# A new order for the steps of the attention section of a fused attention and feed-forward block

## The chip, the cores and the metric

The kernel runs on one core of one Trainium2 chip. The metric is the time of one execution on the device in microseconds (us); lower is better. Times of one kernel are given as the median of several runs. A profile is a record of one further execution.

## The reference

Input x has 32 sequences of 64 tokens with 1024 features (2048 tokens), in float32. The block is an attention layer followed by a feed-forward layer, each with a conditioning layer ahead of it:

```
x = x + attn(cond(x, itok_B_0_2))       # cond: W plus a low-rank delta chosen per sequence
x = x + ffn(cond2(x, itok_B_0_7))       # cond2 and ffn: a base matrix plus top-2 of 8 low-rank experts
```

What matters here is `attn`, with 32 query heads and 8 key and value heads of width 32:

```
qkv = x @ w_qkv.T + b_qkv
q, k, v = split(qkv);  q, k = rope(q), rope(k);  k, v repeated 4 times
scores = q @ k.T / sqrt(32), masked causally
out = softmax(scores) @ v
return out @ w_o.T + b_o
```

## The kernel before

The 2048 tokens are worked on in two halves of 1024 (`hf` 0 and 1); the code is the same for both. Activations lie with features on the 128 partitions and tokens along the free axis. Large matrix products are done in seven block products where eight would be usual (Strassen's scheme in Winograd's form). A `Group` (line 213 on) is one such product of 256 output features by 1024 tokens. It owns three PSUM banks x, y and z, and its steps are:

- on TensorE (PE): `m1` and `m2` into x; `m6`, `m7` and `m4` into y; `p5` and `m3` into z. With the long inner dimension (`qk` groups) a step is four matmuls of 128x512, with the short one (`o` groups) two. In the trace a float32 matmul is two records, so eight or four.
- between them the banks are read: `e1` (ScalarE, ACT) copies x after `m1`; `e6` and `e7` (VectorE, DVE) add y to that copy after `m6` and `m7`, before the next product is added into y; `out11` reads z after `p5` and before `m3`; `out00`, `out01` and `out10` read the finished x, z and y.

The section that the change touches lies at the end of attention: the last `qk` groups (g = 5 holds the values; `held` is the group before it, whose last output is still open), and the first half of the output projection (`o_pairs`, `pairs[0]` to `pairs[3]`). Woven into these are eight units of attention (`u` = 0 to 7, one of two head groups with one of four sets of sequences), each with a chain of steps over two half units (`two` = 0, 1):

- `scores(u)`: 32 small matmuls on 32x32 tiles of TensorE (L1383) into four banks; `flipped(u, two)`: DVE transposes two banks into a tile `e` (L1409); `shaded`: POOL (GpSimd) adds the mask (L1416); `topped`: DVE takes the maxima (L1428); `lowered`: POOL subtracts a maximum (L1433); `exponentials`: ACT (L1446, L1449); `totalled`: DVE sums and takes reciprocals (L1454, L1455); `divided`: POOL multiplies (L1460); `turned`: DVE transposes the weights (L1472) into a tile that `in_place_of(j)` takes over from the column sums of `x`.
- `v_turned(c, i)`: four transposes of the values on TensorE (L1364), and `v_out`: ACT copies them; `values(us)`: 64 small matmuls (L1483, tiles `av`) for two units; `valued_out`: four copies on ACT (L1498) into `q`.
- `o_sums`: column sums on DVE for the projection; `to_x[...].pop(...)()`: POOL adds a result to x; `o_load(G, p)`: four transfers of projection weights on SP's queue. `g.some`, `held.out01` and the `more` in an `out` issue the low-rank matmuls of L434 on 32 rows.

The whole section stands in `with tc.manual_schedule()`: each engine's queue, that of PE, DVE, ACT, POOL and SP, has its instructions in the order of the calls. Semaphores guard the data between engines, and an engine that waits holds up all that is queued behind it. `ps_tile` is a pool of five PSUM banks (scores, `av`, some banks of groups), `group_bank` one of three.

A matmul step and a read-out, and the place of the tile that `turned` writes:

```
def m6(self):
    self.y = self.bank("y")
    self.mult(self.y, "s2", "t2", True)
def e6(self):
    self.add01 = self.sum("u1")
    nc.vector.tensor_add(self.add01, self.y, self.add10)
...
def in_place_of(j, name):
    return xt.pool.tile([P, 4, 512], F32, tag=f"sum{j - 1}", name=f"{name}_{hf}")
```

Of the kernel before, what the change touches and what calls it, by code (L numbers as in the profile page):

```python
# [77 lines left out]
def block_kernel(ctx: ExitStack, tc: tile.TileContext, a, out: bass.AP):  # L78
# [1176 lines left out]
    for hf in range(2):  # L1255
# [212 lines left out]
        def turned(u, two, j=None):  # L1468
            if two == 0:
                to = in_place_of(j, f"ws{u}").rearrange("p j k -> p (j k)")[:, : 48 * HB]  # L1470
                ws[u] = to, to.rearrange("p (j m k) -> p j m k", j=4, m=4)
            nc.vector.transpose(ws[u][0][:, two * 24 * HB : (two + 1) * 24 * HB], units[u][two])  # L1472
# [111 lines left out]
        with tc.manual_schedule():  # L1584
# [42 lines left out]
            flipped(2, 1)  # L1627
            topped(2, 0)
            shaded(2, 1)
            topped(2, 1)  # L1630
# [3 lines left out]
            scored[3] = scores(3)  # L1634
            g.e7()
            g.some((0, 0), (1, 0), held=held)
            turned(1, 0, 3)
            turned(1, 1)
            flipped(3, 0)
            g.m4()  # L1640
            exponentials(2, (0,))
            exponentials(2, (1,))
            flipped(3, 1)
            totalled(2, 0)
            g.out(0, 0, g.x, None)
            shaded(3, 0)
            totalled(2, 1)
            shaded(3, 1)
            topped(3, 0)
            g.part("p5", (0, 1))  # L1650
            g.part("p5", (2, 3))
            divided(2, 1)
            lowered(3, 0)
            exponentials(3, (0,))
            g.out10()
# [12 lines left out]
            wo0 = o_load(0, 0)  # L1668
            rotated()
            turned(2, 0, 4)  # L1670
            totalled(3, 0)
            turned(2, 1)
            totalled(3, 1)
            divided(3, 0)
            g.part("p3", (0, 1))
            g.some((0, 1))
            g.part("p3", (2, 3))
            valued_out((0, 1))
            g.out01()
            scored[4] = scores(4)  # L1680
            v_turned(1, 0, group_bank)
            v_turned(1, 1, group_bank)
            divided(3, 1)
            turned(3, 0, 1)
            flipped(4, 0)
            flipped(4, 1)
            turned(3, 1)
            shaded(4, 0)
            shaded(4, 1)
            topped(4, 0)  # L1690
            topped(4, 1)
            lowered(4, 1)
            v_out(1, 0)
# [5 lines left out]
            v_out(1, 1)  # L1699
            pairs[0].m1()  # L1700
            pairs[0].e1()
            values((2, 3))
# [24 lines left out]
            pairs += o_pairs(0, 1, wo1, ot, (group_bank, group_bank), to_x[1])  # L1727
            pairs[0].e6()
            totalled(4, 1)
            divided(4, 1)  # L1730
            topped(5, 0)
            pairs[1].out00()
            pairs[2].m1()
            scored[6] = scores(6)
            pairs[0].m7()
            pairs[0].p5()
# [4 lines left out]
            o_sums(0, t0, 0, (3,))  # L1741
            o_sums(0, t0, 1, (3,))
            shaded(5, 1)
            lowered(5, 0)
            topped(5, 1)
            exponentials(5, (0,))
            totalled(5, 0)
            divided(5, 0)
            lowered(5, 1)
            pairs[0].m3()  # L1750
            pairs[0].out01()
            pairs[2].e1()
            exponentials(5, (1,))
            flipped(6, 0)
            pairs[0].m4()
# [11 lines left out]
            pairs[1].m7()  # L1767
            flipped(7, 0)
            turned(5, 1)
            flipped(7, 1)  # L1770
            topped(6, 0)
            shaded(6, 1)
            pairs[1].e7()
            pairs[1].out11()
            topped(6, 1)
            shaded(7, 0)
            to_x[0].pop((0, 1, 0))()
            lowered(6, 1)
            topped(7, 0)
# [5 lines left out]
            pairs[1].out10()  # L1785
            pairs[1].out01()
            shaded(7, 1)
            to_x[0].pop((0, 0, 1))()
            lowered(6, 0)
            exponentials(6, (0,))  # L1790
            totalled(6, 0)
            pairs[2].p5()
            pairs[2].e6()
            pairs[2].m7()
            divided(6, 0)
            to_x[0].pop((0, 1, 1))()
            turned(6, 0, 4)
            pairs[2].e7()
            wo0 = o_load(1, 0)
            pairs[3].m1()  # L1800
            lowered(7, 0)
            exponentials(6, (1,))
            exponentials(7, (0,))
            topped(7, 1)
            lowered(7, 1)
            exponentials(7, (1,))
            pairs[3].e1()
            valued_out((4, 5))
            pairs[2].out11()
            totalled(6, 1)  # L1810
            pairs[2].m4()
            pairs[2].m3()
            pairs[2].out10()
            pairs[3].m6()
            totalled(7, 0)
            divided(6, 1)
            divided(7, 0)
            pairs[3].e6()
            pairs[2].out01()
            totalled(7, 1)  # L1820
            pairs[3].m2()
            pairs[3].out00()
            turned(6, 1)
            turned(7, 0, 1)
            pairs[3].p5()
            pairs[3].m7()
            to_x[0].pop((1, 0, 1))()
            divided(7, 1)
            turned(7, 1)
            values((6, 7))  # L1830
# [9 lines left out]
            o_sums(1, t1, 1, (0,))  # L1840
            o_sums(1, t1, 0, (1,))
            o_sums(1, t1, 1, (2,))
            o_sums(1, t1, 1, (1,))
            pairs[3].out01()
            o_sums(1, t1, 1, (3,))
            pairs[3].out10()
            o_sums(1, t1, 0, (3,))
            to_x[1].pop((0, 0, 1))()
            to_x[1].pop((1, 0, 1))()
            to_x[1].pop((0, 1, 0))()  # L1850
            to_x[1].pop((0, 1, 1))()
            to_x[0].pop((1, 1, 0))()
            to_x[0].pop((1, 1, 1))()
            to_x[1].pop((1, 1, 0))()
            to_x[1].pop((1, 1, 1))()
# [372 lines left out]
```

## Time and profile before

| what | us |
|---|---|
| median of 4 runs (lowest to highest) | 1128.46 (1127.76 to 1128.64) |
| the profiled execution, its own time | 1128.69 |
| its span, first to last instruction | 1126.8 |
| TensorE busy in the span | 1115.6 |
| the section in half one, roughly 410 to 546: PE, DVE, POOL, ACT busy of 136 | 135.0, 98.6, 85.9, 51.9 |
| the section in half two, roughly 836 to 975: PE, DVE, POOL, ACT busy of 139 | 136.5, 98.3, 84.0, 51.8 |
| granted TensorE clock over the span | 1.00 |

Busy time is that of instructions at work, without waiting. PEld is the weight load of TensorE, which overlaps its matmuls. In a list of waits a line names who waited, for whom, the total in us, how often, and the longest. In a timeline a line has the start and length in us, the engine, the source line, the operation, output and inputs by tile names, the shape, the number of records, and in brackets the engine's idle time ahead of it with what ended it. "issue" stands where no semaphore explains the wait.

### The profile page before, as it was taken

The page shows a single profiled execution, that of the slowest core. Times are in us where ns is not written, and L with a number is a line of the kernel's source. Part 1 is how long each engine was busy: PE and PEld are TensorE (multiplying, and loading weights), DVE is VectorE, ACT ScalarE, POOL GpSimd, SP SyncE. Part 2 cuts the span into 40 slices and gives each one's busy share as a digit, 9 for nine tenths or more (in the row PEclk, how much of TensorE's full clock was granted, in tenths as well). Part 3 has the DMA queues.
Part 4 walks back from the last instruction along what each step waited for, and adds up shares of the span by engine and source line. Part 5 has one row for each costly group of instructions (what it writes and reads, how often), then busy time and mean ns, then how long its engine had stood idle before and what let it go on. Part 6 is the DMA issues. An engine that isn't in the chain of part 4 may idle for free.

```text
span 1126.8 us, 15708 instructions
## 1 busy us (share of the span) xinstructions
PE 1115.6 (99%) x5974; PEld 625.5 (56%) x5974; DVE 721.0 (64%) x1279; ACT 191.3 (17%) x736; POOL 549.9 (49%) x530
## 2 busy tenths in 40 slices
PE   9999999999999999999999999999999999999998
PEld 4555555555444444444458887444444444458887
DVE  4879853749445787973946565344767864847654
ACT  1101001000000426450000000000225550011000
POOL 5877586550532665647405651111545556602333
PEclk9999999999999999999999999999999999999999
DMA  9312773969322232032116669222222024113454
GB/s 321 122 38 94 284 248 135 337 210 323 118 74 75 75 113 77 8 123 98 33 48 194 202 193 310 77 75 75 75 75 76 2 76 135 50 36 98 148 150 145
DMA packets 115147, 144.99 MB, mean 129 GB/s; under 512 B 6912, under 2 KB 92928, under 8 KB 113024
## 3 DMA queue, kind: packets, MB, share of 16 engines
q1 hardware_dynamic: 103168, 113.99, 31.3%
q0 software_dynamic: 4848, 19.93, 5.0%
q10 hardware_dynamic: 7056, 10.07, 2.5%
q8 instruction: 47, 0.77, 0.3%
q14 instruction: 28, 0.23, 0.1%
HBM read 102.97 MB, written 41.00 MB: 128 GB/s over the span
## 4 chain that ended last, share of the span: by engine, by line
PE 96%; DVE 2%; DMA 1%; POOL 1%; issue 1%; ACTq 0%; POOLq 0%; DVEq 0%
PE qk_y L272 11%; PE o_y L272 7%; PE qk_z L272 7%; PE qk_x L272 7%; PE f_y L272 6%; PE o_x L272 5%; PE o_z L272 5%; PE cqp_y L596 4%; PE f_z L272 4%; PE f_x L272 4%; PE cf_y L272 4%; PE cqp_z L596 3%; PE cqp_x L596 3%; PE cf_z L272 2%; PE cf_x L272 2%; PE f_z L284 2%
## 5 line engine op out<-in xcount | busy, mean ns | idle before, releaser
L1302 POOL TENSOR_TENSOR t<-raw,consts 128x512 f32<-128x512 f32 x40 | 57.6, 1445 | 130.0 <-DVE q L1301 78.6
L1446 ACT ACTIVATE e<-e,top 128x64 f32<-128x64 f32 x256 | 85.2, 336 | 87.1 <-DVE top L1428 87.1
L272 PE MATMUL qk_y<-sum_x,s_qk 128*128 128x512 f32 x192 | 86.8, 595 | 0.0
L272 PE MATMUL qk_x<-x,w_qk 128*128 128x512 f32 x192 | 86.6, 594 | 0.0
L272 PE MATMUL f_y<-s_f,w_f 128*128 128x256 f32 x336 | 82.3, 380 | 0.3 <-DVE f_u L327 0.3
L1460 POOL TENSOR_TENSOR e<-e,tot 128x256 f32<-128x256 f32 x64 | 52.0, 835 | 40.9 <-DVE tot L1455 40.8
L272 PEld LDWEIGHTS f_y<-s_f,w_f 128*128 128x128 f32 x336 | 63.8, 190 | 9.3 <-DVE f_u L327 0.7
L1416 POOL TENSOR_TENSOR e<-e,consts 128x512 f32<-128x512 f32 x32 | 40.9, 1294 | 52.3 <-DVE e L1409 52.3
L272 PEld LDWEIGHTS qk_y<-sum_x,s_qk 128*128 128x128 f32 x192 | 36.1, 190 | 45.5 <-issue 43.7
L272 PEld LDWEIGHTS qk_x<-x,w_qk 128*128 128x128 f32 x192 | 36.3, 190 | 44.9 <-issue 44.4
L272 PE MATMUL o_x<-q,w_o 128*128 128x512 f32 x128 | 59.4, 598 | 0.2 <-issue 0.2
L1446 ACT ACTIVATION_READ_ACCUMULATOR e<-e,top 128x1 f32 x256 | 48.4, 189 | 0.0
L1222 POOL COPY gatesr<-oh1r 128x1024 f32<-128x1024 f32 x4 | 4.1, 1036 | 86.8 <-DVE oh1r L1220 86.8
L272 PE MATMUL qk_y<-sum_x,w_qk 128*128 128x512 f32 x96 | 44.4, 606 | 0.0
L272 PE MATMUL qk_z<-x,s_qk 128*128 128x512 f32 x96 | 43.9, 597 | 0.0
L272 PE MATMUL qk_z<-sum_x,s_qk 128*128 128x512 f32 x96 | 43.4, 595 | 0.0
L272 PEld LDWEIGHTS o_x<-q,w_o 128*128 128x128 f32 x128 | 23.7, 190 | 28.4 <-issue 27.4
L596 PE MATMUL cqp_y<-t_p,s_p 128*128 128x384 f32 x112 | 38.7, 489 | 0.5 <-POOL s_p L708 0.4
L1334 DVE SCALAR_TENSOR_TENSOR raw<-qk_z,consts,qk_u 128x512 f32<-128x512 f32 (+1 forms) x28 | 18.3, 664 | 31.8 <-PE qk_z L434 27.8
L1409 DVE STREAM_TRANSPOSE e<-sc 128x384 f32<-128x384 f32 x64 | 32.0, 550 | 9.8 <-PE sc L1383 9.4
L296 ACT COPY f_p<-f_x 128x256 f32<-128x256 f32 x28 | 10.4, 372 | 159.6 <-PE f_x L272 117.8
L1311 DVE TENSOR_TENSOR q<-q,t 128x512 f32<-128x512 f32 x32 | 31.2, 976 | 9.0 <-POOL t L1302 9.0
(407 smaller groups left out, 2414.1 us busy)
## 6 DMA issues: line engine op xcount, KB each, us to landing
w_f<-cf SPq DMA_DIRECT2D x28, 512.0 KB, 4.3
w_qk<-cqkv SPq DMA_DIRECT2D x12, 1024.0 KB, 5.5
w_f<-cf SPq DMA_DIRECT2D x28, 384.0 KB, 4.5
x<-in_xT SPq DMA_DIRECT2D x16, 512.0 KB, 5.8
w_o<-in_wo SPq DMA_DIRECT2D x16, 512.0 KB, 4.6
s_o<-wos SPq DMA_DIRECT2D x16, 512.0 KB, 5.8
sqk<-s_qk POOLq DMA_DIRECT2D x6, 1024.0 KB, 4.2
outT<-o ACTq DMA_DIRECT2D x20, 256.0 KB, 4.1
```

The costliest lines, as they stand in the source:

```text
L272: self.last = nc.tensor.matmul(ps, self.weights[left][:, kc, :], self.right(right, kc), start=first and kc == 0, stop=kc == self.h - 1, sk ...
L284: nc.tensor.matmul(ps, lhs, rhs, start=False, stop=True, skip_group_check=True)
L296: nc.scalar.copy(self.add10, self.x)
L596: nc.tensor.matmul(ps, self.weights[left][kc], self.right(right, kc), start=first and kc == 0, stop=kc == self.h - 1, skip_group_check=True,)
L1222: nc.gpsimd.tensor_copy(gates, oh1.unsqueeze(3).to_broadcast([P, NT, E, R]))
L1302: nc.gpsimd.tensor_mul(t2v, rv, c3)
L1311: nc.vector.tensor_add(*unfinished.pop())
L1334: nc.vector.scalar_tensor_tensor(to, ps, bias, add, ALU.add, ALU.add)
L1409: nc.vector.transpose(e[:, 12 * HB * i : 12 * HB * (i + 1)], scored[u][2 * two + i][:, : 12 * HB])
L1416: nc.gpsimd.tensor_add(diagonal, diagonal, upper)
L1446: nc.scalar.activation(es[1][:, n], es[1][:, n], AF.Exp, bias=top[:, 1, n : n + 1], accum_out=tot[:, 1, n : n + 1])
L1460: nc.gpsimd.tensor_mul(es[i], es[i], wide(tots[u][two][:, i], (i + 1) * HB))
```

## The change

The same calls are made in another order. Nothing else is changed: the same instructions, tiles and banks. On TensorE's queue the order changes at five places in each half:

1. `scores(2)` stands ahead of `g.m6()` instead of behind it, and `g.m2()` ahead of `flipped(2, 0)` and `g.e6()`.
2. `v_turned(0, 1)` stands next to `v_turned(0, 0)`, ahead of the low-rank matmul of `g.out11()` (in `g.some((1, 1))`).
3. `scores(5)` stands ahead of `pairs[0].m2()` and `pairs[1].m2()` instead of between them.
4. `pairs[1].p5()` stands ahead of `scores(7)` and `pairs[2].m2()`.
5. `pairs[1].m3()` stands behind `pairs[2].m6()`.

The other moves are on DVE, ACT and POOL. The diff, cut to the parts with these moves and the ones around them:

```diff
             g.m1()
+            scored[2] = scores(2)
             g.m6()
-            scored[2] = scores(2)
             g.e1()
             turned(0, 0, 2)
+            turned(0, 1)
+            g.m2()
+            flipped(2, 0)
             g.e6()
-            turned(0, 1)
-            flipped(2, 0)
-            g.m2()
+            flipped(2, 1)
             shaded(2, 0)
-            flipped(2, 1)
             topped(2, 0)
...
             v_turned(0, 0, group_bank)
+            v_turned(0, 1, ps_tile)
+            v_out(0, 0)
             held.out01()
-            v_out(0, 0)
+            v_out(0, 1)
             g.some((1, 1))
-            v_turned(0, 1, ps_tile)
             divided(2, 0)
-            g.out11()
             topped(3, 1)
             lowered(3, 1)
-            v_out(0, 1)
+            g.out11()
+            exponentials(3, (1,))
             values((0, 1))
-            exponentials(3, (1,))
+            valued_out((0, 1))
...
             valued_out((2, 3))
+            o_sums(0, t0, 0, (0,))
             o_sums(0, t0, 1, (0,))
-            o_sums(0, t0, 0, (0,))
-            o_sums(0, t0, 1, (1,))
+            o_sums(0, t0, 0, (1,))
             o_sums(0, t0, 1, (2,))
             lowered(4, 0)
+            scored[5] = scores(5)
+            o_sums(0, t0, 1, (1,))
+            pairs[1].e1()
             pairs[0].m2()
-            scored[5] = scores(5)
-            flipped(5, 0)
-            o_sums(0, t0, 0, (1,))
-            shaded(5, 0)
-            pairs[1].e1()
             pairs[1].m2()
             pairs[0].m6()
+            pairs[0].out00()
+            flipped(5, 0)
+            shaded(5, 0)
             flipped(5, 1)
-            pairs[0].out00()
...
             flipped(6, 1)
+            pairs[1].p5()
+            pairs[1].e6()
             scored[7] = scores(7)
             pairs[2].m2()
-            pairs[1].p5()
-            shaded(6, 0)
-            pairs[1].e6()
+            pairs[1].m7()
             totalled(5, 1)
...
             pairs[2].out00()
             values((4, 5))
             pairs[1].m4()
-            pairs[1].m3()
             pairs[2].m6()
             pairs[1].out10()
+            pairs[1].out11()
+            pairs[1].m3()
+            lowered(6, 0)
+            shaded(7, 0)
+            shaded(6, 1)
+            topped(6, 1)
+            pairs[2].p5()
...
             values((6, 7))
-            pairs[3].e7()
+            pairs[3].m4()
             pairs[3].out11()
-            pairs[3].m4()
+            pairs[3].out00()
             pairs[3].m3()
+            to_x[1].pop((1, 1, 1))()
```

`pairs[0].m7()`, `pairs[0].p5()`, `turned(4, 0, 4)`, `pairs[0].e7()`, `turned(4, 1)`, `pairs[0].out11()`, `o_sums(0, t0, 0, (3,))`, `o_sums(0, t0, 1, (3,))` and `shaded(5, 1)` keep their order; `pairs[0].m3()` follows them at once in the new order.

More of the change, by code (lines that the diff above doesn't have):

```diff
@@ L1636, in block_kernel @@
             g.some((0, 0), (1, 0), held=held)
+            g.m4()
             turned(1, 0, 3)
+            flipped(3, 0)
             turned(1, 1)
-            flipped(3, 0)
-            g.m4()
             exponentials(2, (0,))
+            totalled(2, 0)
+            shaded(3, 0)
             exponentials(2, (1,))
+            g.out(0, 0, g.x, None)
             flipped(3, 1)
-            totalled(2, 0)
-            g.out(0, 0, g.x, None)
-            shaded(3, 0)
             totalled(2, 1)
@@ L1651, in block_kernel @@
             g.part("p5", (2, 3))
+            lowered(3, 0)
+            g.out10()
             divided(2, 1)
-            lowered(3, 0)
             exponentials(3, (0,))
-            g.out10()
             v_turned(0, 0, group_bank)
+            v_turned(0, 1, ps_tile)
+            v_out(0, 0)
             held.out01()
-            v_out(0, 0)
+            v_out(0, 1)
             g.some((1, 1))
-            v_turned(0, 1, ps_tile)
             divided(2, 0)
-            g.out11()
             topped(3, 1)
             lowered(3, 1)
-            v_out(0, 1)
+            g.out11()
+            exponentials(3, (1,))
             values((0, 1))
-            exponentials(3, (1,))
+            valued_out((0, 1))
             wo0 = o_load(0, 0)
+            turned(2, 0, 4)
             rotated()
-            turned(2, 0, 4)
+            turned(2, 1)
             totalled(3, 0)
-            turned(2, 1)
             totalled(3, 1)
-            divided(3, 0)
             g.part("p3", (0, 1))
@@ L1677, in block_kernel @@
             g.part("p3", (2, 3))
-            valued_out((0, 1))
+            scored[4] = scores(4)
             g.out01()
-            scored[4] = scores(4)
             v_turned(1, 0, group_bank)
             v_turned(1, 1, group_bank)
+            v_out(1, 1)
+            v_out(1, 0)
+            divided(3, 0)
+            flipped(4, 0)
+            turned(3, 0, 1)
+            flipped(4, 1)
             divided(3, 1)
-            turned(3, 0, 1)
-            flipped(4, 0)
-            flipped(4, 1)
+            shaded(4, 0)
             turned(3, 1)
-            shaded(4, 0)
-            shaded(4, 1)
             topped(4, 0)
-            topped(4, 1)
-            lowered(4, 1)
-            v_out(1, 0)
             two = [in_place_of(j, f"sums_o{j}") for j in (2, 3)]
@@ L1698, in block_kernel @@
             pairs = o_pairs(0, 0, wo0, ot, (group_bank, group_bank), to_x[0])
-            v_out(1, 1)
+            shaded(4, 1)
+            topped(4, 1)
+            lowered(4, 1)
             pairs[0].m1()
@@ L1726, in block_kernel @@
             divided(4, 0)
-            pairs += o_pairs(0, 1, wo1, ot, (group_bank, group_bank), to_x[1])
+            totalled(4, 1)
             pairs[0].e6()
-            totalled(4, 1)
             divided(4, 1)
@@ L1732, in block_kernel @@
             pairs[1].out00()
+            lowered(5, 0)
+            exponentials(5, (0,))
+            pairs += o_pairs(0, 1, wo1, ot, (group_bank, group_bank), to_x[1])
             pairs[2].m1()
+            pairs[2].e1()
             scored[6] = scores(6)
@@ L1743, in block_kernel @@
             shaded(5, 1)
-            lowered(5, 0)
+            pairs[0].m3()
+            totalled(5, 0)
             topped(5, 1)
-            exponentials(5, (0,))
-            totalled(5, 0)
-            divided(5, 0)
+            pairs[0].out01()
             lowered(5, 1)
-            pairs[0].m3()
-            pairs[0].out01()
-            pairs[2].e1()
             exponentials(5, (1,))
             flipped(6, 0)
+            divided(5, 0)
+            shaded(6, 0)
             pairs[0].m4()
@@ L1766, in block_kernel @@
             turned(5, 0, 1)
-            pairs[1].m7()
             flipped(7, 0)
@@ L1770, in block_kernel @@
             flipped(7, 1)
+            pairs[1].e7()
             topped(6, 0)
[L1772 to L1779, printed above, removed]
+            shaded(7, 1)
             pairs[2].out00()
@@ L1782, in block_kernel @@
             pairs[1].m4()
-            pairs[1].m3()
             pairs[2].m6()
             pairs[1].out10()
+            pairs[1].out11()
[5 more added lines that the diff above has]
+            pairs[2].p5()
+            topped(7, 0)
+            pairs[2].e6()
+            topped(7, 1)
             pairs[1].out01()
-            shaded(7, 1)
+            pairs[2].m7()
             to_x[0].pop((0, 0, 1))()
-            lowered(6, 0)
+            to_x[0].pop((0, 1, 0))()
+            lowered(6, 1)
+            lowered(7, 0)
+            to_x[0].pop((0, 1, 1))()
+            pairs[2].e7()
+            pairs[2].out11()
+            wo0 = o_load(1, 0)
+            pairs[3].m1()
+            lowered(7, 1)
             exponentials(6, (0,))
             totalled(6, 0)
-            pairs[2].p5()
-            pairs[2].e6()
-            pairs[2].m7()
             divided(6, 0)
[L1796 to L1801, printed above, removed]
             exponentials(6, (1,))
             exponentials(7, (0,))
-            topped(7, 1)
-            lowered(7, 1)
-            exponentials(7, (1,))
             pairs[3].e1()
             valued_out((4, 5))
-            pairs[2].out11()
+            pairs[2].m4()
+            pairs[2].out10()
             totalled(6, 1)
-            pairs[2].m4()
             pairs[2].m3()
-            pairs[2].out10()
             pairs[3].m6()
             totalled(7, 0)
-            divided(6, 1)
-            divided(7, 0)
-            pairs[3].e6()
+            to_x[0].pop((1, 0, 1))()
+            exponentials(7, (1,))
+            turned(6, 0, 4)
             pairs[2].out01()
@@ L1821, in block_kernel @@
             pairs[3].m2()
-            pairs[3].out00()
+            pairs[3].p5()
+            divided(7, 0)
+            divided(6, 1)
+            turned(7, 0, 1)
+            pairs[3].e6()
+            pairs[3].m7()
             turned(6, 1)
[L1824 to L1827, printed above, removed]
             divided(7, 1)
             turned(7, 1)
+            pairs[3].e7()
             values((6, 7))
-            pairs[3].e7()
+            pairs[3].m4()
             pairs[3].out11()
-            pairs[3].m4()
+            pairs[3].out00()
             pairs[3].m3()
+            to_x[1].pop((1, 1, 1))()
             t1 = [ep.tile([P, 1024], F32, tag="e", name=f"sumo{hf}{j}") for j in range(4)]
@@ L1840, in block_kernel @@
             o_sums(1, t1, 1, (0,))
+            o_sums(1, t1, 1, (1,))
             o_sums(1, t1, 0, (1,))
-            o_sums(1, t1, 1, (2,))
-            o_sums(1, t1, 1, (1,))
+            o_sums(1, t1, 1, (3,))
             pairs[3].out01()
-            o_sums(1, t1, 1, (3,))
             pairs[3].out10()
             o_sums(1, t1, 0, (3,))
-            to_x[1].pop((0, 0, 1))()
+            o_sums(1, t1, 1, (2,))
             to_x[1].pop((1, 0, 1))()
             to_x[1].pop((0, 1, 0))()
+            to_x[1].pop((1, 1, 0))()
+            to_x[0].pop((1, 1, 1))()
+            to_x[1].pop((0, 0, 1))()
             to_x[1].pop((0, 1, 1))()
             to_x[0].pop((1, 1, 0))()
-            to_x[0].pop((1, 1, 1))()
-            to_x[1].pop((1, 1, 0))()
-            to_x[1].pop((1, 1, 1))()
             ot = Columns(o_columns(1), 512, 2, [[t[:, kc, :] for kc in range(2)] for t in t1])
```

## The prediction

> **What bounds the kernel now.** I read first the busy shares and the chain that ended last, then who TensorE waited for, then TensorE's own timeline in the two stretches that the change touches (one per half of the tokens).
>
> ```profile
> PE 1115.6 (99%) x5974; PEld 625.5 (56%) x5974; DVE 721.0 (64%) x1279; ACT 191.3 (17%) x736; POOL 549.9 (49%) x530
> ...
> q8 instruction: 47, 0.77, 0.3%
> ...
> PE 96%; DVE 2%; DMA 1%; POOL 1%; issue 1%; ACTq 0%; POOLq 0%; DVEq 0%
> ```
>
> TensorE is busy 1115.6 of 1126.8 us and is 96% of the chain. A new order neither adds nor removes a matmul, so it can win only what TensorE loses now between them. The waits of TensorE, the longest first, as totals, times and longest:
>
> ```profile
> PE o_z L272 <- DVE o_u L1570: 1.7, 2, 0.8
> PE av L1483 <- issue: 1.7, 1, 1.7
> PE idle L135 <- DVE idle L132: 1.2, 1, 1.2
> PE cqp_z L596 <- POOL s_p L702: 1.0, 1, 1.0
> ...
> PE o_x L272 <- issue: 0.2, 1, 0.2
> ```
>
> Only three of these lie in the reordered section: 1.7 + 1.7 + 0.2 = 3.6 us, 0.3% of the span. That is the ceiling of any gain. The timeline (start, length, what, records) shows where they lie; a matmul of 512 columns is two records.
>
> ```profile
> 428.87 0.60 PE L1364 MATMUL v<-consts,raw 128*128 128x128 f32 x4
> 429.40 1.12 PE L434 MATMUL qk_z<-low,b1q 32*128 32x512 f32 x2
> 430.45 0.66 PE L1364 MATMUL v<-consts,raw 128*128 128x128 f32 x4
> 431.04 2.33 PE L1483 MATMUL av<-ws,v 32*32 32x256 f32 x128
> ...
> 442.13 2.33 PE L1483 MATMUL av<-ws,v 32*32 32x256 f32 x128
> 444.39 0.70 PE L272 MATMUL o_x<-q,w_o 128*128 128x512 f32 x1
> ...
> 460.81 1.98 PE L272 MATMUL o_z<-q,s_o 128*128 128x512 f32 x4 [0.85 <-DVE o_u L1570]
> ...
> 869.05 2.19 PE L1483 MATMUL av<-ws,v 32*32 32x256 f32 x113
> 872.90 0.45 PE L1483 MATMUL av<-ws,v 32*32 32x128 f32 x15 [1.66 <-issue]
> ```
>
> Back to back, a group of four records takes 1.72 us (480.22 to 481.94) and one of eight 3.43; a group next to small tiles takes 0.10 more (411.35 to 412.56 is one block of scores, 1.21 us; the group before it runs 407.82 to 411.35 = 3.53).
>
> **The o_z wait stays.** `p5` fills a bank, `out11` (L1570) must empty it, `m3` fills it again. In the new order `m7, p5, e7, out11, m3` of `pairs[0]` stand as before, with the same second `turned(4)` ahead of `out11` on DVE. 0 us; if it went after all, -0.85 in each half.
>
> **The "issue" waits are code arriving.** Queue q8 moves 0.77 MB in 47 packets, 16 KB each; TensorE's 5974 matmul and 5974 load records with its 155 queue instructions make 12,100, so an instruction is 64 bytes and a packet 256 of them. Counted in program order, the wait of half one comes before instruction 4287 (the second weight load of an `o_x`) and that of half two near 9408: 5,121 apart, 20 packets. In the trace's DMA records a q8 packet starts at 442.90 and TensorE goes on at 445.27, 2.37 later; the other starts at 870.49 and TensorE goes on at 872.90, 2.41 later. So the next 256 instructions are usable 2.4 us after their transfer starts, and an `av` block eats 256 in 2.26 us. The cost now: 444.39 to 448.47 (two groups of four) is 4.08 against 3.63 for such groups, 0.45 lost; 869.05 to 873.28 is 4.23 against 2.26, 1.97 lost. In half two the transfer starts late because the weight loads fill the queues ahead of it:
>
> ```profile
> q1 hardware_dynamic: 333, 1.24, 94.1%
> ...
> w_o<-in_wo SPq DMA_DIRECT2D x1, 512.0 KB, 5.4
> s_o<-wos SPq DMA_DIRECT2D x1, 512.0 KB, 7.5
> ```
>
> (the DMA view cut to 866.0 to 870.4: data packets take 94%, and no code packet runs.) The Trainium skill, "Runtime: NRT & Kernel Launch", section "Instruction fetch mechanics", has 16 KiB blocks of 256 instructions, as here, but calls a crossing "mostly hidden". By it, the code term below would be 0 and my sum 0.47 lower; the rows above show 0.45 and 1.97, so the rows decide.
>
> **The change part by part, per half.** Counts of compute and DMA instructions are unchanged on every engine; only places move.
>
> (1) `scores(2)` goes ahead of `g.m6()`. The 1.21 us block only changes places, and small tiles stand between large ones as before: 0. But `e6` loses cover. `turned(0, 0)` overwrites the column sums that `m6` reads (`in_place_of(2)`), so DVE now begins it when `m6` ends, with this queue ahead of `e6`:
>
> ```profile
> 411.46 0.98 DVE L1472 STREAM_TRANSPOSE ws<-e 128x768 f32<-128x768 f32 x1 [0.36 <-PE qk_y L272]
> 412.36 0.65 DVE L309 TENSOR_TENSOR qk_u<-qk_y,qk_p 128x512 f32<-128x512 f32 x1
> ```
>
> Before, one transpose stood ahead of `e6`, and TensorE had `scores(2)` and `m2` to run (1.21 + 3.53) before `m7` needed the bank back. Now: about 0.2 from `m6`'s last start to DVE's start, two transposes at 0.90 (0.98 less the overlap with the next), two half flips at 0.46, `e6` at 0.65: 3.6 us, against 3.43 for `m2`. `m7` waits 0.16. The bounds: 0 (each step 5% faster) and 0.35 (5% slower). I take 0.16, so +0.32 for both halves. Queued behind `m7` is all of TensorE; nobody else waits.
>
> (2) `v_turned(0, 1)` goes ahead of the `L434` of `out11`, next to `v_turned(0, 0)`. TensorE changes tile size v, 434, v, av (three changes) before; v, 434, av (two) now. A change costs 0.09: the group before scores takes 3.53, not 3.43. The trace never shows `L434` straight before `av`; bounds 0 and 0.19 saved (two changes, if 32-row tiles follow each other free). Scores straight before `L434` (419.63 to 420.84) cost the same 1.21 as scores before large tiles, so the size of the columns counts too: I take 0.09, -0.18 for both halves.
>
> (3) `scores(5)` goes ahead of `pairs[0].m2()`. Its banks are freed by the four copies of `valued_out((2, 3))`, which take 2.05 us from 444.45 to 446.50; its fourth tile needs the third copy, done some 1.6 us after `av`, and `m1` plus the change lasts 1.82. Margin 0.1 to 0.2: 0 us; gone, it would cost that copy's 0.5.
>
> (4) `pairs[1].p5()` goes ahead of `scores(7)` and `pairs[2].m2()`; `pairs[1].m3()` goes behind `pairs[2].m6()`, and `out11` behind `out10` on DVE. From the end of `m4`: 0.2, `out10` 0.67, `out11` 0.75, 0.05 to TensorE: 1.67 against the 1.72 of `m6`. Margin 0.05: 0 us; at worst it loses an L1570 row, 0.75.
>
> (5) Everything else (masks, maxima, exponentials, `divided`, `o_sums`, `to_x`, `out00`) moves on DVE, ACT and POOL, busy 98.6, 51.9 and 85.9 of the 136 us from 410 to 546. Followed instruction by instruction with the durations of the trace, every TensorE wait in the new order but (1) and the old `o_z` ends before TensorE comes to it, the closest by 0.04 to 0.26 us. 0 us, with (3) and (4) as what is lost if the cover goes. On SP the `o_load` transfers keep their order and hang on matmuls that move by under 0.2 us; one transfer of `o_load(1, 0)` comes an `m3` later, 1.7, some 15 us before it is used.
>
> (6) Code. The built program has two more queue instructions on TensorE ahead of `av(2,3)` in half one and four in half two. The `av` block begins at instruction 4030, not 4028, so the packet border falls before the first weight load of the `o_x` after it, not its second. The code is there at the same moment, but 0.43 of work (one record) is no longer done before it: 0.88 lost, not 0.45, +0.43. In half two the border stays inside the block, four instructions earlier: +0.04. Bounds: -2.4 (both waits gone) to +3.65 (the request of half one held up as in half two, where it starts 4.40 after the border and not 0.75).
>
> The sum: +0.32 - 0.18 + 0.47 = +0.61 us on the profiled execution's 1128.69 (span 1126.8 and 1.9 around it), 1129.3. The median of the runs, 1128.46, lies 0.23 below the profiled one: 1129.1.
>
> **The rivals.**
> A. The border of code falls kindlier in half two, say the transfer starts two us earlier, and that 1.97 goes: 1129.1 - 2.0 = 1127.1. For it: in half one a transfer started among the same loads without delay. Against: loads and border keep their distance in the new order to within 0.05 us. With half one's wait gone too, 1126.2, on the 0.2% line: the only way there.
> B. Slower: in half one the code request stands behind the 1.5 MB of `o_load(0, 1)`, as in half two. Place: the border at `av(2,3)`, loads issued 3.8 us before it. Price 3.65: 1132.8. It decides once the transfer starts over 2.3 us later than at 442.90. Against: the same distance gave no delay before.
> C. The thin margins fail: 0.5 for (3), 0.75 for (4), in both halves +2.5, 1131.6; one of them, 1130.0. For: DVE rows here vary (1.43 and 1.75 at 408.00 and 409.35 where others of their lines take 0.69). Against: POOL and ACT idle a third and more of the stretch.
> D. The `o_z` wait goes: 1129.1 - 1.7 = 1127.4. Against: its five steps are untouched.
>
> **How the numbers follow.** My forecast 0.60; A 0.12, a third of it past 0.2%; B 0.07; C 0.15, a fifth of it past; D 0.06. 0.2% is 2.3 us, about what a measurement of this kernel can tell from no change: faster 0.04, slower 0.07 + 0.03 = 0.10, within 0.86. The range 1126.9 to 1131.0 holds the forecast, D, A by half one's wait kept, and most of C, and leaves B out.
>
> **What would show it.** TensorE's idle time before `qk_y` (`m7`) near 416 and 843: 0.1 to 0.2 from DVE. `o_z` still 0.85 twice. The `o_x` after `av` near 444 starting 0.9 late, the `av` near 871 still broken for some 1.7. `v`, `L434` and `av` near 429 to 431 shorter by 0.1. I am wrong if TensorE shows a wait above 1 us in the section that is not one of these, or if the chain leaves TensorE for ACT or POOL.

## The result, and the profile after

| | before | after |
|---|---|---|
| median of the runs, us | 1127.79 (52 runs) | 1130.14 (32 runs) |
| ratio to before, 95% interval | | 1.0023 (1.0015 to 1.0030) |
| the profiled execution, and its span | 1128.69, 1126.8 | 1132.06, 1130.3 |

The new order is about 2.4 us slower. The time lies in the forecast range and the interval straddles the 0.2% line, but the forecast of 1129.1, a loss of 0.61, was about a quarter of the loss measured. The first and fourth part of the profiled page after, cut to the busy times of the engines and their shares of the chain that ended last:

```profile
PE 1117.7 (99%) x5974; PEld 625.9 (55%) x5974; DVE 724.7 (64%) x1279; ACT 190.9 (17%) x736; POOL 550.7 (49%) x530
...
PE 93%; DVE 2%; POOL 2%; DMA 1%; issue 1%; SPq 0%; ACTq 0%; POOLq 0%; DVEq 0%
```

TensorE still bounds the kernel. Its busy time has grown by 2.1 us with the same 5974 matmuls, so some of them ran slower. The waits of TensorE after, by total, times and longest:

```profile
PE av L1483 <- issue: 2.5, 1, 2.5
PE o_z L272 <- DVE o_u L1570: 1.7, 2, 0.8
...
PE o_x L272 <- issue: 1.2, 1, 1.2
```

The two waits for code have grown from 1.7 to 2.5 and from 0.2 to 1.2; the `o_z` wait is as it was. TensorE's timeline after, half one and then half two:

```profile
403.47 3.60 PE L272 MATMUL qk_x<-x,w_qk 128*128 128x512 f32 x8
...
411.75 3.60 PE L272 MATMUL qk_x<-x,w_qk 128*128 128x512 f32 x8
415.44 3.67 PE L272 MATMUL qk_y<-sum_x,s_qk 128*128 128x512 f32 x8
...
428.28 1.04 PE L1364 MATMUL v<-consts,raw 128*128 128x128 f32 x8
429.25 1.12 PE L434 MATMUL qk_z<-low,b1q 32*128 32x512 f32 x2
430.30 2.33 PE L1483 MATMUL av<-ws,v 32*32 32x256 f32 x128
...
441.39 2.33 PE L1483 MATMUL av<-ws,v 32*32 32x256 f32 x128
444.89 1.98 PE L272 MATMUL o_x<-q,w_o 128*128 128x512 f32 x4 [1.17 <-issue]
...
464.38 1.88 PE L272 MATMUL o_y<-sums_o,s_o 128*128 128x512 f32 x4
...
840.44 3.60 PE L272 MATMUL qk_x<-x,w_qk 128*128 128x512 f32 x8
844.04 3.70 PE L272 MATMUL qk_y<-sum_x,s_qk 128*128 128x512 f32 x8
...
870.02 2.18 PE L1483 MATMUL av<-ws,v 32*32 32x256 f32 x111
874.73 0.46 PE L1483 MATMUL av<-ws,v 32*32 32x128 f32 x17 [2.53 <-issue]
875.11 3.56 PE L272 MATMUL o_x<-q,w_o 128*128 128x512 f32 x4
```

`m2` to `m7` takes 3.69 in half one (411.75 to 415.44) and 3.60 in half two (840.44 to 844.04) where 3.43 is back to back: the `e6` wait, 0.26 and 0.17. DVE's timeline after has `e6` end at 415.29, 0.15 ahead of `m7`:

```profile
414.64 0.65 DVE L309 TENSOR_TENSOR qk_u<-qk_y,qk_p 128x512 f32<-128x512 f32 x1
```

`v` to `av` takes 2.02 where it took 2.17. The last line of TensorE's timeline is new: a group of four takes 3.56 and not 1.88. The stretches of the windows view show why (start and end, length, busy time and instructions of PE, PEld, DVE, ACT and POOL, granted clock, DMA share, GB/s):

```profile
868.00:872.00 4.00, 4.00 (x119) 2.39 (x117) 4.00 (x8) 1.66 (x3) 2.55 (x2) 1.00 0.97 345
872.00:875.00 3.00, 0.47 (x27) 0.19 (x17) 0.85 (x2) 0.00 (x0) 1.19 (x2) 1.00 0.11 36
875.00:879.00 4.00, 4.00 (x53) 1.31 (x37) 1.68 (x3) 2.35 (x5) 0.00 (x0) 0.57 0.02 4
879.00:883.00 4.00, 4.00 (x72) 1.94 (x41) 2.51 (x5) 4.00 (x23) 0.00 (x0) 1.00 0.00 0
```

After the long wait TensorE's granted clock is 0.5 for one stretch of 3.413 us (from 875.38), 0.57 on average over 875 to 879. At half speed half of that stretch is lost, 1.7 us.

From `g.m1` of g = 5 to `pairs[1].m6` (403.47 to 464.38 in half one), half one takes 60.91 after and 59.95 before, half two 64.08 and 61.47: +3.57 in this pair of executions, as much as the span has grown (3.5). Outside this stretch the differences cancel in sum, but they are not all small: `lgrows` (L1927, matmuls on x for the feed-forward layer) behind the projection of half one takes 5.44 after and 4.16 before (from its start to the group `h_x`), and the kernel ahead of the section is 0.92 shorter. The experiment with four instructions comes back to `lgrows`.

### The profile page after: what moved, and what is told of

The parts are those of the page before. It is cut to its first block, busy times and chain, and to the rows that moved or that the text cites. A ratio compares the mean times of both kernels' runs of the same rounds, so it can differ in the third digit from the quotient of the medians.

```text
span 1130.3 us, 15699 instructions
## 1 busy us (share of the span) xinstructions
PE 1117.7 (99%) x5974; PEld 625.9 (55%) x5974; DVE 724.7 (64%) x1279; ACT 190.9 (17%) x736; POOL 550.7 (49%) x530
## 4 chain that ended last, share of the span: by engine, by line
PE 93%; DVE 2%; POOL 2%; DMA 1%; issue 1%; SPq 0%; ACTq 0%; POOLq 0%; DVEq 0%
PE qk_y L272 11%; PE qk_z L272 7%; PE qk_x L272 7%; PE o_y L272 6%; PE f_y L272 6%; PE o_x L272 5%; PE cqp_y L596 4%; PE f_z L272 4%; PE f_x L272 4%; PE o_z L272 4%; PE cf_y L272 4%; PE cqp_z L596 3%; PE cqp_x L596 3%; PE cf_z L272 2%; PE cf_x L272 2%; PE f_z L284 2%
```

## The experiments

Two theories. T1: the loss comes from the code for the end of `av(2,3)` and what its lateness sets off; the order's own waits are small. T2: the order's own waits and thin margins cost the 2.4 us.

**Less weight data ahead of the code.** In the first load of each half, `o_load(0,0)`:

```diff
+            def sums():
+                for i in range(2):
+                    nc.sync.dma_start(s[:, i], wos[:, 4 * G + 2 * p + i])
+
+            if (G, p) == (0, 0):
+                for i in range(2):
+                    nc.sync.dma_start(w[:, i], a["wo"][2 * p + i, :, G * H : (G + 1) * H, :])
+                late["o_sums"] = sums
+                return w, s
...
             with tc.issue_after(pairs[1].last.ins):
+                late["o_sums"]()
                 wo1 = o_load(0, 1)
```

> Edit: the two 0.5 MB transfers of s_o in the first o_load of each half are issued behind the w_o ones, and only after av(2,3), so that less weight data stands ahead of the code packet that TensorE waits for in half two's av block. T1 (the loss is code delivery at av(2,3)): the 1.66 us wait inside half two's av block falls to at most 0.9; half one's 0.2 before o_x stays within 0.5; 1127 us, about 1 us (0.999) faster than before. T2 (the loss is the order's own waits and margins): this kernel has none of them, so no change: 1128.0, ratio 0.9995 to 1.0005.

> The same edit in the changed order. T1: the 2.53 us wait in half two's av falls to at most 0.9, the stretch of halved clock from 875.4 on goes, and the changed order ends at most 0.8 us above before_s_late: about 1127.8, ratio to before 0.9995 to 1.0005. T2: the order's own waits are untouched, so it stays 2 to 2.5 us above before_s_late.

Measured: 0.9997 (0.9981 to 1.0013) and 1.0014 (0.9997 to 1.0031). The edit missed its aim: the traces show the transfers of `o_load(0,0)` at 401 to 405 and 828 to 832, while the three that start ahead of `av(2,3)` are those of `o_load(0,1)`, which wait on SP's queue for their buffers and not for the call's place. Near `av(2,3)` these two kernels are repeats of the unmodified ones, and so they show how much the code wait varies:

```profile
869.17 2.19 PE L1483 MATMUL av<-ws,v 32*32 32x256 f32 x113
873.87 0.45 PE L1483 MATMUL av<-ws,v 32*32 32x128 f32 x15 [2.51 <-issue]
874.25 5.40 PE L272 MATMUL o_x<-q,w_o 128*128 128x512 f32 x8
```

This is half two of the timeline in the old order: the same wait of 2.5, and the same slow `o_x` behind it (5.40 for eight records that take 3.70). In the new order with the edit it was 0.89. So the long wait and the halved clock occur in both orders.

**The borders moved away.** At the kernel's start, 192 more TensorE instructions:

```diff
-    for n in (256, 256, 256):
+    for n in (256, 256):
         nc.tensor.matmul(ps[:, :n], idle[:, :P], idle[:, :n], start=True, stop=True)
+    for n in range(49):
+        r = slice(n % 4 * 32, n % 4 * 32 + 32)
+        nc.tensor.matmul(ps[r, :16], idle[r, :32], idle[r, :16], start=True, stop=True)
```

> Edit: 96 more tiny matmuls' worth of TensorE instructions (192) at the start of the kernel, in place of one of the three idle matmuls, so that every border between code packets falls 192 instructions earlier in the program's steps: no border lies within av(2,3) of either half any more, but others fall at other steps. T1: the two waits at av(2,3) (0.45 and 1.97 us lost) go; 1126 us, ratio 0.998, unless a border falls in another burst of small matmuls, which would show as an issue wait there. T2: no change from before, ratio 0.9995 to 1.0005.

> The same edit in the changed order. T1: both code waits at av(2,3) go, no stretch of halved clock near 875, and the changed order ends within 0.3 us of before_plus192 (the e6 wait of 0.16 and 0.07 less the 0.15 saved at v and L434 per half): 1126 us, ratio to before about 0.998. T2: it stays 2 to 2.5 us above before_plus192.

Measured: 0.9977 (0.9962 to 0.9992) and 0.9983 (0.9968 to 0.9999). Neither `av(2,3)` waits any more, in either half. (One statement of the expectation is wrong: a border still lies in `av(2,3)`, 64 instructions in for half one and 29 for half two, in the new order. But the border ahead of that one is some 190 to 230 instructions before `av`, so the code behind it was fetched long before: its transfer starts 8.3 and 8.8 us ahead of `av`.) The two orders are now 0.7 us apart by these ratios. Half one of the new order still lost 0.57, since the next border fell 48 instructions into the moved `scores(5)` (timeline of the new order with 192 more):

```profile
446.31 1.98 PE L275 MATMUL o_x<-q,w_o 128*128 128x512 f32 x4
448.23 1.85 PE L1386 MATMUL sc<-q,k 32*32 32x256 f32 x64
```

The code transfer had started at 446.42, so it was usable near 448.8; the block takes 1.28 elsewhere. Without this wait the stretch from `g.m1` to `av(6,7)`, in which all five moves lie, is 0.07 longer in the new order than in the old, both halves together.

**The loads moved behind the code.** Of `o_load(0,1)` the last three transfers go to ACT's queue, after `exponentials(4, (1,))`:

```diff
+            def loads(queue, i):
+                queue.dma_start(w[:, i], a["wo"][2 * p + i, :, G * H : (G + 1) * H, :])
+                queue.dma_start(s[:, i], wos[:, 4 * G + 2 * p + i])
+
+            if (G, p) == (0, 1):
+                nc.sync.dma_start(w[:, 0], a["wo"][2 * p, :, G * H : (G + 1) * H, :])
+                def rest():
+                    nc.scalar.dma_start(s[:, 0], wos[:, 4 * G + 2 * p])
+                    loads(nc.scalar, 1)
+                late["o_rest"] = rest
+                return w, s
...
             exponentials(4, (1,))
+            late["o_rest"]()
```

> Edit: of the second projection load, o_load(0,1), the three transfers (1.5 MB) that start 3.9 us ahead of av(2,3) go to ACT's queue behind exponentials(4, (1,)), about 453 and 880, so that no weight data moves while the code for the end of av(2,3) is fetched; they are first needed some 17 us later. T1 (half two's code packet is held up by these loads): the packet of half two starts within 1.2 us of the border before it, the 1.7 to 2.5 us wait inside half two's av falls under 0.3, no halved clock; half one's wait before o_x stays 0.2 to 0.5. 1.7 to 2 us faster, ratio 0.998. T2 (the code comes late for another reason, or the loss is in the order's own waits): the wait in av stays at 1.7 to 2.5, ratio 0.9995 to 1.0005.

> The same edit in the changed order. T1: half two's av unbroken (wait under 0.3), no halved clock near 875; the wait before half one's o_x stays at 0.9 to 1.9; it ends 0.4 to 1 us above before_load_late (half one's border, the e6 waits, less the saving at v and L434): ratio to before 0.999. T2: it stays 2 to 2.5 us above before_load_late.

Measured: 0.9972 (0.9962 to 0.9983) and 0.9984 (0.9972 to 0.9997). Half two in the new order, timeline and then the DMA view from 866.0 to 870.4 (first line packets and bytes, then each queue's packets, MB and share of 16 engines):

```profile
870.16 2.33 PE L1483 MATMUL av<-ws,v 32*32 32x256 f32 x128
872.42 1.98 PE L272 MATMUL o_x<-q,w_o 128*128 128x512 f32 x4
```
```profile
DMA packets 1, 0.02 MB, mean 4 GB/s; under 512 B 0, under 2 KB 0, under 8 KB 0
...
q8 instruction: 1, 0.02, 1.5%
```

In the changed kernel the same stretch of time holds 0.91 MB of weights and no code packet:

```profile
DMA packets 239, 0.91 MB, mean 207 GB/s; under 512 B 17, under 2 KB 17, under 8 KB 239
...
q1 hardware_dynamic: 239, 0.91, 70.2%
```

With the loads out of the way both code waits are gone in both halves. That half one's would go as well I had not expected. The starts of the code transfers, from the DMA records, against the start of `av(2,3)` show why (negative: ahead of it; the wait is TensorE's, in or behind `av(2,3)`):

| kernel | half one: start, wait | half two: start, wait | halved clock |
|---|---|---|---|
| before | +0.77, 0.18 | +1.44, 1.66 | no |
| before_s_late | +0.99, 0.46 | +2.35, 2.51 | yes |
| after | +1.24, 1.17 | +2.36, 2.53 | yes |
| after_s_late | +1.82, 1.93 | +0.71, 0.89 | no |
| after_again (below) | +0.76, 0.75 | -0.54, none | no |
| before_plus4 (below) | +0.90, 0.96 | +1.45, 1.66 | no |
| after_less4 (below) | +1.70, 0.62 | +2.09, 2.23 | yes |
| before_load_late | -1.18, none | -2.18, none | no |
| after_load_late | -1.73, none | -2.20, none | no |

Without loads the transfer starts 1.2 to 2.2 us before the block; with them 1.7 to 4.6 us later than that, a different amount in each execution. In all thirteen waits of the table TensorE goes on 2.26 to 2.44 us after the transfer's start. So it is shown that the loads hold up the code and that this makes the waits at `av(2,3)`. T2 does not fit the profiles: with the code out of the way, `g.m1` to `pairs[1].m6` takes 59.66 and 59.60 in the new order and 59.51 and 59.50 in the old, 0.25 us for both halves; up to `av(6,7)`, with moves (4) and (5), 0.10 is left. The ratios put the two kernels 1.35 us apart, with over 1 us to either side of each, so they alone would not exclude T2. In the two profiles `lgrows` in half one takes 5.45 in the new order and 4.39 in the old, which would be most of that distance.

**Four TensorE instructions more or fewer.** One more tiny matmul in the old order, and two idle matmuls of 384 columns for three of 256 in the new one:

```diff
+    nc.tensor.matmul(ps[:32, :16], idle[:32, :32], idle[:32, :16], start=True, stop=True)
```
```diff
-    idle = tmp("idle")[:, :256]
+    idle = tmp("idle")[:, :384]
...
-    for n in (256, 256, 256):
+    for n in (384, 384):
```

> Edit: one more tiny matmul (four TensorE instructions) at the start of the kernel in the old order, so that the packet borders lie in both halves where the new order has them, to two instructions (half one: at instruction 255 of the block from the start of av(2,3), against 257 in the new order and 259 in the old; half two: 222 as in the new order, against 226). T1a (the place of the border carries the whole difference): as slow as the changed kernel, ratio 1.002. T1b (the place costs only what I forecast): half one's wait rises from 0.2 to 0.5 to 0.9 to 1.2, half two's stays in its 0.9 to 2.5, ratio 1.0004. T2 (the order's own waits): 1.0000.

> Edit: two idle matmuls of 384 columns at the start in place of three of 256, four TensorE instructions fewer in the new order; borders at 261 (half one) and 226 (half two), as in the old order to two instructions. T1a: as fast as the old order, ratio 1.000. T1b: half one's wait falls to 0.2 to 0.5, half two's stays in its 0.9 to 2.5, ratio 1.0015. T2: 1.0023 as the changed kernel.

Measured: 1.0010 (1.0001 to 1.0019) and 1.0006 (0.9996 to 1.0016). The timelines of half one, first the old order with four more, then the new with four fewer:

```profile
442.84 2.31 PE L1484 MATMUL av<-ws,v 32*32 32x256 f32 x127
446.12 0.26 PE L1484 MATMUL av<-ws,v 32*32 32x128 f32 x1 [0.96 <-issue]
```
```profile
445.67 1.12 PE L272 MATMUL o_x<-q,w_o 128*128 128x512 f32 x2
447.41 1.12 PE L272 MATMUL o_x<-q,w_o 128*128 128x512 f32 x2 [0.62 <-issue]
```

The stop moves with the border, to the last record of `av` or behind two records of `o_x`, as the count of instructions says. The old order with the new one's borders is 1.1 us slower; the new order with the old borders, at 1.0006, lies under the 1.0018 to 1.0023 of the changed kernel. Four instructions at the start of the kernel, with no change of order, so cost the old order about half of what the whole change did (between 0.1 and 2.1 us by the interval); the ratios do not tell T1a and T1b apart.

The profiles show one place more. `lgrows` in half one, from its start to `h_x`, takes 5.19 in the old order with four more, and 4.90 to 5.45 in the four profiles of the new order whose instruction count ahead of it is unchanged (after, after_s_late, after_load_late, after_again). In the other nine, the new order with four fewer (4.33) among them, it takes 4.16 to 4.39. Counted from the trace, 5638 or 5640 TensorE instructions stand ahead of it in the five long cases, 5634 or 5636 in seven of the short ones and some 192 more in two. So about 1 us goes with the place of the borders, at a step behind the reordered section. Lines of the changed kernel, POOL's and TensorE's, and then POOL's line in the old order:

```profile
530.30 1.27 POOL L182 TENSOR_TENSOR s_h<-w_h 128x512 f32<-128x512 f32 x1 [2.38 <-DMA w_h<-cffn]
...
553.42 1.90 PE L1927 MATMUL lgrows<-x,wr 128*32 128x512 f32 x10 [0.28 <-DVE x L1572]
```
```profile
528.79 1.26 POOL L182 TENSOR_TENSOR s_h<-w_h 128x512 f32<-128x512 f32 x1 [0.83 <-DMA w_h<-cffn]
```

The load of `w_h`, issued at 523.05 and 523.09, holds POOL up 1.5 us longer, and the last of DVE's additions into x, for which TensorE waits, comes 1.2 later (552.68 and 551.44). POOL starts this step 6.6 to 7.3 us after the issue in the five long cases and 5.7 to 5.9 in the other nine. Why the place of the borders should do this, no run shows.

**The changed kernel once more.** No edit.

> The changed kernel itself once more, beside the two below on one chip: 1.0020 to 1.0028. T1: its profile shows the wait before o_x in half one (0.9 to 1.9) and the one inside av in half two (0.9 to 2.5); if the latter is over 2 us and lies within one stretch of 3.413 us counted from the first rise of the clock, a stretch of halved clock follows it.

Measured: 1.0018 (1.0005 to 1.0031). The profile missed what was expected of it: the code wait of half two did not occur, and half one's was 0.75 (span 1125.3, against 1130.3). A single profile shows one draw: from `g.m1` to `pairs[1].m6`, both halves together, the old order took 121.42 and 124.24 (before, before_s_late) and the new one 124.99, 122.46 and 120.08 (after, after_s_late, after_again), so these differ by more within an order than the 2.4 us between the medians. Over all executions, 16 of 46 of the changed kernel had a mean clock of 0.998 or less, what one halved stretch makes of it, and 14 of 97 of before. Of the kernels without code waits at `av(2,3)` (the borders or the loads moved) 1 of 60 had. The kernel best, below, is left out of these: 4 of its 6 had, and it has waits of 2.04 of its own. On this chip executions with such a clock took 1132.9 and the others 1129.6; before took 1131.6 and 1128.7.

**The new order without move (1).** With the loads late as above:

```diff
             g.m1()
-            scored[2] = scores(2)
             g.m6()
+            scored[2] = scores(2)
             g.e1()
             turned(0, 0, 2)
+            g.e6()
             turned(0, 1)
-            g.m2()
             flipped(2, 0)
-            g.e6()
-            flipped(2, 1)
+            g.m2()
             shaded(2, 0)
+            flipped(2, 1)
```

> The new order with the three late loads of after_load_late, and with move (1) undone: scores(2) behind m6, e6 behind one transpose, as in the old order. The e6 wait then goes: in the profile m2 to m7 takes 3.4 to 3.6 with scores in between and no wait, 0.26 us per half less than in after_load_late, 0.5 us in all; v, L434 and av keep their saving of 0.15 per half. T1: 1127.0 if before_load_late is at 1127.1 on this chip, ratio to before 0.997. T2 (some other wait of the order): it stays at after_load_late's 0.9984.

Measured: 0.9978 (0.9966 to 0.9990). The timeline of half one:

```profile
410.41 1.28 PE L1383 MATMUL sc<-q,k 32*32 32x256 f32 x64
411.62 3.70 PE L272 MATMUL qk_x<-x,w_qk 128*128 128x512 f32 x8
415.15 3.60 PE L272 MATMUL qk_y<-sum_x,s_qk 128*128 128x512 f32 x8
```

`m2` to `m7` is 3.53, the length of a group next to small tiles. The ratio's interval holds both forecasts, 0.997 and 0.9984; the profile decides. `g.m1` to `pairs[1].m6` falls to 59.33 and 59.33: 0.33 and 0.27 less than with move (1), and 0.18 and 0.17 less than the old order with the loads late, which is the saving at `v` and L434.

**Away with the o_z wait, twice.** First `m4` as cover for `out11`, then `pairs[2].m2`:

```diff
+            pairs[0].m4()
             pairs[0].m3()
...
-            pairs[0].m4()
             pairs[1].m6()
-            pairs[0].out10()
             flipped(6, 1)
+            pairs[0].out10()
```

> after_ll_e6 and one more move: pairs[0].m4 ahead of pairs[0].m3 (with flipped(6, 1) ahead of out10 on DVE), so that m4 runs while DVE empties the bank z. T1: the two o_z waits of 0.84 go, no new wait above 0.3 before scores(7): 1.5 us under after_ll_e6, ratio to before 0.9955 to 0.996. The other way: scores(7) waits for flipped(6, 1), and up to 0.5 of each 0.84 comes back there: ratio 0.9965.

```diff
-            exponentials(5, (0,))
             pairs[2].e1()
+            exponentials(5, (0,))
...
+            pairs[2].m2()
             pairs[0].m3()
...
+            totalled(5, 1)
+            divided(5, 1)
             flipped(6, 1)
...
-            pairs[2].m2()
             pairs[1].m7()
-            totalled(5, 1)
-            divided(5, 1)
             turned(5, 0, 1)
-            flipped(7, 0)
             turned(5, 1)
+            flipped(7, 0)
```

> after_ll_e6 with another cover for the o_z wait, in place of the one that failed in best: pairs[2].m2, whose operands are there, runs between pairs[0].p5 and m3, while DVE empties z; for it e1 of pairs[2] goes ahead of exponentials(5, (0,)) on ACT, totalled(5, 1) and divided(5, 1) ahead of flipped(6, 1), and turned(5, 1) ahead of flipped(7, 0). T1 (the wait is only a missing cover): both o_z waits of 0.84 go and no other wait above 0.3 takes their place: 1.6 us under after_ll_e6, ratio to before 0.9963. The other way: m2 or m7 waits (for e1, or for e6 behind the moved totals), up to 0.8 each half, ratio 0.998 as after_ll_e6.

The first was 1.0051 (1.0034 to 1.0068), a miss in both its cases. Its waits:

```profile
PE o_y L272 <- DVE sums_o L203: 4.1, 2, 2.0
PE o_y L272 <- DVE o_u L1582: 1.7, 2, 0.8
...
PE o_z L272 <- DVE o_p L1582: 1.1, 2, 0.5
```

`m4` reads the last column sums, which DVE makes after `out11`, so the cover itself waited 2.04 in each half; then `pairs[1].m6` waited for the bank that `out01` frees and `p5` for the one that `out10` frees. The second was 0.9956 (0.9941 to 0.9971), the fastest of all: 1123.85 against 1128.18 for before. The longest of its waits, with no `o_z` among them; all lie outside the section:

```profile
PE idle L135 <- DVE idle L132: 1.2, 1, 1.2
PE cqp_z L596 <- POOL s_p L702: 0.7, 1, 0.7
PE h L525 <- issue: 0.5, 1, 0.5
```

From `g.m1` to the first matmul of the group `h` behind attention the halves take 148.33 and 148.73, against 149.13 and 149.48 without this edit.

## Why the prediction was right, and where it was too small

The sign, the bound and the places were right. That the time fell into the range was in part luck: the range was wide enough for rival C, which did not come, and what filled it was late code, whose large form (rival B) the range left out.

- The bound: right. TensorE sets the time, and what changed lies in its gaps and, in the profiled execution, in one stretch of halved clock.
- The `o_z` wait: right, 0.84 twice in the changed kernel. That it is only a missing cover, best2 shows.
- (1) the `e6` wait: right in place and cause, too small. Forecast 0.16 a half; `m2` to `m7` shows 0.26 in half one and 0.17 in half two. The sum did not have that `m7` itself then takes 3.60 and 3.63 and not 3.53; undoing the move gives back 0.33 and 0.27.
- (2) the tile sizes: right in sign. 0.15 a half at `v` (0.17 to 0.18 by the section), forecast 0.09.
- (3) and (4), the margins: they held. The one slow `scores(5)` seen (1.85) was code, not a late copy. Together the order's own part is 0.25 us up to `pairs[1].m6` with the code out of the way, and 0.07 to 0.10 up to `av(6,7)`; the same terms of the forecast sum to 0.14.
- (6), code: this step failed in size, though its mechanism is the cause. "The code is there at the same moment" does not hold: the transfer starts at a moment that changes from execution to execution, from 0.76 to 1.82 us after the start of `av(2,3)` in half one of the new order and from 0.54 before to 2.36 after in half two. I had taken one execution's 0.75 and 4.40 for constants. Forecast 0.43 for half one; the waits there are 0.75, 1.17 and 1.93 in three profiles of the new order, against 0.18 and 0.46 in two of the old. Forecast 0.04 for half two; in the profiled pair it cost 0.87 more waiting and 1.7 of halved clock, a cost that the sum did not have at all. Nor did it have the 1 us at `lgrows`, which goes with the same borders.
- Rival B stood nearest, and after_again's half two, without a wait, is what rival A had: both are draws of the same transfer. Its condition in half one, a start "over 2.3 us later", was not reached (at most 1.05 later, +1.82 against +0.77), but the argument against it, that "the same distance gave no delay before", was wrong: with the loads moved away half one's transfer starts 1.95 us earlier in the old order, so it had been delayed all along, by just little enough to hide.

What stays open: why the transfer is held up longer in one execution than in another, and why `w_h` holds POOL up longer with the borders in their new place. The shares of the 2.4 us are read from profiles, a single one of most kernels; the intervals of the run times are too wide to confirm them.

## What to carry to other kernels

Where TensorE runs a burst of small matmuls, count its instructions and see where the 256-instruction borders fall; keep bulk loads from being issued in the few us before such a burst, or move them to where large matmuls give the code time. A change of order that adds a handful of queue instructions moves all later borders, so compare two orders with the code waits taken out, and judge a wait that depends on transfers by several executions and not by one profile. A block can cover a wait only if its own operands are ready: look at what it reads before placing it.

## What was not expected of the hardware

The clock. The halved stretches of three profiles start at the same moment, 870.40 us after the first rise of the clock, which is 255 stretches of 3.4133 us. Laid on that grid, waits of 2.23, 2.51 and 2.53 us that fell wholly within one stretch were each followed by one at half clock; a wait of 2.95 us in before_load_late (near 698.7) that the grid cuts into 1.17 and 1.78 was not, nor was one of 1.82. So where a wait falls counts as well as its length; between 1.82 and 2.23 idle within one stretch lies the limit that these runs show. In all fourteen traces, no other stretch of the grid ahead of the last matmul's holds more than 1.82 us without a matmul, and none of them is followed by half clock. The Trainium skill, "TensorE: Matmul & The Clock Gate", Part 1, describes the window as 3413 ns long and free-running, which agrees; its section on oscillation gives the rule as no idle gaps above about 3.4 us, where here 2.23 was enough.

The code. "Runtime: NRT & Kernel Launch", section "Instruction fetch mechanics", has the next page fetched while the current one runs, and the crossing mostly hidden. At `av(2,3)` it was hidden in every kernel whose loads or borders were moved; with 1.5 MB of loads issued 3.9 us ahead of the burst it was not, by up to 2.5 us.
